# Softplus as one ScalarE function in a planned selective-scan block, with the planner's priorities shifted

## The chip, the core and the metric

The kernel runs on one core of a Trainium2 chip. The core has a matrix engine (TensorE, PE in the profile; PEld is its weight load), VectorE (DVE), ScalarE (ACT), GpSimd (POOL) and SyncE (SP), whose queue issues all DMAs here. The metric is the device time of one execution in microseconds; before the change it is 3109.58 us (median of 3 runs, 3109.41 to 3114.28).

## The reference, cut to what matters

The input x is 2 sequences of 2048 tokens with 1024 channels, float32 throughout. Three blocks follow each other, each on a layernorm of x and added to x: a routed feed-forward block (FFN 1), a selective scan with 16 states per channel, and the same feed-forward block again (FFN 2).

```python
xz = jnp.einsum('btd,rd->btr', x, W_xproj)
delta_r, B_mat, C_mat = xz[..., :r], xz[..., r:r + n], xz[..., r + n:]
delta = jax.nn.softplus(jnp.einsum('btr,dr->btd', delta_r, W_dt) + b_dt)
A = -jnp.exp(A_log)
dA = jnp.exp(delta[..., None] * A)
Bu = delta[..., None] * B_mat[:, :, None, :] * x[..., None]
# scan over t: h = dA_t * h + Bu_t;  y_t = sum_n h * C_t
return y + x * D_param
```

`delta` holds the step sizes of the title: one per token and channel. The feed-forward block forms 64 vectors of rank 16 per token (`vecs`), keeps the 4 longest, and adds their product with a second weight to x W + bias.

## The kernel before, in words

Tokens are worked in 16 chunks of 256 (`TC`), each chunk in two tiles of 128 rows for the FFNs. `ffn("f", c, i)` is FFN 1 of tile i of chunk c, `ffn("g", c, i)` is FFN 2. An FFN tile has three stages of products on TensorE, each 2 halves x 8 matmuls of 128x512 (`products`, line 578; each float32 matmul leaves two records in the profile): with `wa` into two PSUM banks `pv`, with `ww` into two banks `po`, and with `wb` into the same `po`. Between the first and the last stand the squares (ACT, line 631), the choice (`choose`, `routed`, `total`; DVE, lines 645 to 668), `spread` (POOL, line 677), eight transposes on TensorE (line 560) and the copies that bring them to SBUF (ACT, line 565, tile `gt`). `close` (DVE, line 695) adds the result to x. The layernorm is folded in: the weights wa and ww are centred once at the start, and the row's own scale comes in `close`, from `stats` (DVE, lines 512 to 527) and `root` (ACT, lines 532 to 534).

`prepare(c)` normalises and transposes the chunk, projects it, and computes `delta`. Here lie the lines that the change touches. For each half g of the channels (32 groups in all) four matmuls (`pz`, line 797) give z in two PSUM banks, taken one after the other. Then comes softplus(z) = max(z, 0) + ln(1 + exp(-|z|)), with a term that keeps what rounding loses in 1 + e: Abs and Relu on ACT out of PSUM with the bias of the channel (`parts`, lines 806 and 807), Exp (819), three steps on DVE (`plus` 822, `one` 827, `rest` 830), Ln on ACT (833), and a subtraction on DVE (`delta`, 836). `times` (840) multiplies by u, and two DMAs (856) write delta and delta x u to DRAM. ACT loads a function table whenever the function needed isn't in the active one (ACT_TABLE_LOAD).

`scans(c)` reads them back, repeated over partitions (`rep`), and does 64 steps per chunk: `decay` (Exp on ACT into one of two PSUM buffers `da`, line 917), `entry` (DVE, 925), `scan` (DVE, 932), `keep` (ACT, 942), `leave` and `join` (POOL, 945 and 964), and for each two channel blocks a sum over states on TensorE (974) and `skip` (DVE, 988 and 991).

The order of work is not written by hand: every piece is a `Task` with an engine, a cost, what it reads and writes, and a `rank`. `Plan.order` plays the tasks through in time with these costs. Each engine takes the ready task of the lowest rank that finds its buffers; the order that results is what each engine executes, strictly in that order, waiting on semaphores. A buffer taken with `spare=1` asks for one more free place than it takes. Tasks marked `port` are not planned on DVE and POOL at the same time. There are five PSUM banks in the pool `bank`. FFN 1 runs up to three chunks ahead of the scans.

At the start SyncE loads the transposed x tile (`load_t`), the weights wa, ww, the first x tile in rows (`load`, rank -1006.8), half_bias, wb and the rest (ranks -1009 to -1003). DVE adds the row blocks of wa (`gather`, line 447), POOL those of ww. TensorE turns these sums into column means (`mean`, line 472, rank -1000) and corrects the first tile, whose products use the weights not yet centred (`correct`, 461, rank -1400). DVE subtracts the means (`center`, 482, rank -900).

Of the kernel before, what the change touches and what calls it, by code (L numbers as in the profile page):

```python
# [31 lines left out]

class Place:
# [10 lines left out]
class Task:  # L64
    __slots__ = (
        "eng", "cost", "emit", "rank", "take", "give", "port", "land", "turn", "waits", "users", "n",
        "at",
# [9 lines left out]
class Plan:  # L77
# [15 lines left out]
    def add(  # L93
        self, eng, cost, emit, reads=(), writes=(), rank=0.0, take=(), give=(), port=False, land=0.0,
        turn=None,
    ):
        t = Task()
        t.eng, t.cost, t.emit, t.rank = eng, cost, emit, rank
        t.take, t.give, t.port, t.land, t.turn = take, give, port, land, turn
        t.users, t.n = [], len(self.tasks)  # L100
        before = set()
        for key in reads:
            if key in self.written:
                before.add(self.written[key])
            self.readers.setdefault(key, []).append(t.n)
        for key in writes:
            if key in self.written:
                before.add(self.written[key])
            before.update(self.readers.get(key, ()))
            self.written[key] = t.n  # L110
            self.readers[key] = []
        for p in take:
            p.taker = t.n
        for p in give:
            p.users += 1
        for key in (*reads, *writes):
            if isinstance(key, tuple) and isinstance(key[0], Place):
                before.add(key[0].taker)
        before.discard(t.n)
        t.waits = len(before)  # L120
        for n in before:
            self.tasks[n].users.append(t.n)
        self.tasks.append(t)
        return t

    def order(self):
# [9 lines left out]
        def arrive(t):  # L136
            heapq.heappush(ready[t.eng], (t.rank() if callable(t.rank) else t.rank, t.n))
# [89 lines left out]
def macaron_kernel(  # L227
# [179 lines left out]
    def load_all():  # L407
        def one(dst, src, key, us, rank):
            keys = [(*key, h) for h in range(2)] if isinstance(key, tuple) else [key]
            add("SP", us, lambda: nc.sync.dma_start(out=dst, in_=src), [], keys, rank=rank, land=3.6)  # L410

        def big(w_sb, w, name, rank):
# [10 lines left out]
            rank=-1000.0, take=[mean_w])  # L423
# [17 lines left out]
        for w_sb, name, key in ((wa, "wa", "pv"), (ww, "ww", "po")):  # L441
            total = Place("row" if name == "wa" else "delta")
            for k in range(1, KC):
                def gather(k=k, w_sb=w_sb, total=total):
                    t = flat(total)
                    eng = nc.vector if total.pool == "row" else nc.gpsimd
                    eng.tensor_add(t, w_sb[:, 0, :] if k == 1 else t, w_sb[:, k, :])

                add("DVE" if name == "wa" else "POOL", 1.01 if name == "wa" else 2.45, gather, [(name, 0, 0), (name, k, 0)], [(total, 0)], rank=-1000.0,
                    take=[total] if k == 1 else [], port=True)  # L450
# [17 lines left out]
            for h in range(2):  # L468
                pt = Place("bank")

                def mean(h=h, total=total, pt=pt):
                    nc.tensor.matmul(
                        pt.tile, lhsT=mean_w.tile[:, :P], rhs=flat(total)[:, h * HD : (h + 1) * HD], start=True,
                        stop=True,
                    )

                add("PE", 0.41, mean, [(total, 0), (mean_w, 0)], [(pt, 0)], rank=-1000.0, take=[pt],
                    give=[total, mean_w])
                for k in range(KC):
                    def center(k=k, h=h, w_sb=w_sb, pt=pt):  # L480
                        part = w_sb[:, k, h * HD : (h + 1) * HD]
                        nc.vector.tensor_sub(part, part, pt.tile)  # L482

                    add("DVE", 0.49, center, [(pt, 0)], [(name, k, h)], rank=-900.0, give=[pt])
# [6 lines left out]
            [], ["half_bias"], rank=272.6)  # L491
# [15 lines left out]
    def spread_of(x_p, st, factor, rank, after=()):  # L507
# [28 lines left out]
        add("DVE", 1.95, stats, row(x_p) + list(after), [(st, 0)], rank=-109.8 + rank, take=[st])  # L536
        add("ACT", 2.64, root, [(st, 0)], [(st, 1)], rank=72.4 + rank)
# [14 lines left out]
    def turn(src, keys, dst, out_keys, rank, take=(), give_src=None):  # L552

        for g in range(2):
# [9 lines left out]
            def act(g=g, pt=pt):  # L564
# [4 lines left out]
                give=[src] if give_src else [])  # L569
            add("ACT", 0.58, act, [(pt, 0)], out_keys(g), rank=-111.3 + rank, give=[pt])  # L570
# [3 lines left out]
    def products(turn_of, ps, h, lhs, w, wn, start, stop, order, take, give, after=()):  # L574
        for k4 in range(KC // 4):
            def pe(k4=k4):
# [12 lines left out]
                [(ps[h], 0)], turn=turn_of, rank=order, take=take if k4 == 0 else (), give=give)  # L589

    def ffn(kind, c, i):
# [21 lines left out]
        for h in range(2):  # L613
            def bias(h=h):
                cols = slice(h * HD, (h + 1) * HD)
                nc.gpsimd.tensor_add(x_p.tile[:, cols], x_p.tile[:, cols], half_bias[:, cols])  # L616

            add("POOL", 1.12, bias, row(x_p, h) + ["half_bias"], row(x_p, h), rank=rank, port=True)
# [7 lines left out]
        for h in range(2):  # L626
# [3 lines left out]
            def square(h=h):  # L630
# [7 lines left out]
                take=[g_p] if h == 0 else [])  # L638

        def choose():  # L640
# [14 lines left out]
            take=[ch, mk], give=[mk])  # L655
        for h in range(2):
            def routed(h=h):
# [7 lines left out]
                give=[pv[h]])  # L665
# [7 lines left out]
        add("DVE", 1.2, total, [(g_p, 0), (g_p, 1)], [(ch, 1)], rank=-45.5 + rank)  # L673
        for h in range(2):
            def spread(h=h):
# [8 lines left out]
                give=[ch])  # L684
# [5 lines left out]
        for h in range(2):  # L690
            products(turn_of, po, h, gt, wb, "wb", False, True, lambda: turn_of.number - 1000.0, [], [gt])

            def close(h=h):
# [7 lines left out]
                rank=-286.1 + rank, give=[po[h], st])  # L701
        if kind == "f":
            x1_ds[c, i] = x1_d = Place("x1_d")

            def keep():
# [3 lines left out]
                land=2.5)  # L709
# [11 lines left out]
    def prepare(c):  # L721
# [48 lines left out]
        def keep(p, pt, m):  # L770
# [4 lines left out]
            give=[pd])  # L775
        add("PE", 0.93, project_bc, ["wx"] + u_all, [(pb, 0)], rank=-79.8 + rank, take=[pb])
        add("ACT", 0.46, keep(bc, pb, P), [(pb, 0)], [(bc, 0)], rank=-138.9 + rank, take=[bc],
            give=[pb])
        add("PE", 0.36, fold, [(bc, 0)], [(pf, 0)], rank=91.8 + rank, take=[pf])
        add("ACT", 0.54, keep(bc, pf, 2 * N), [(pf, 0)], [(bc, 0)], rank=104.1 + rank, give=[pf])  # L780
# [8 lines left out]
        for g in range(2):  # L789
            dg, e = Place("delta"), Place("row")  # L790
            for k2 in range(HC // 2):
                pt = Place("bank")

                def pz(g=g, k2=k2, pt=pt):
                    for k in range(2):
                        kc = g * HC + 2 * k2 + k
                        nc.tensor.matmul(  # L797
                            pt.tile[:, k * TC : (k + 1) * TC], lhsT=wdt[:, kc * P : (kc + 1) * P],
                            rhs=dr.tile, start=True, stop=True,
                        )  # L800

                def parts(g=g, k2=k2, pt=pt, e=e, dg=dg):
                    for k in range(2 * k2, 2 * k2 + 2):
                        bias = bdt[:, g * HC + k : g * HC + k + 1]
                        z = pt.tile[:, k % 2 * TC : (k % 2 + 1) * TC]
                        nc.scalar.activation(e.tile[:, k * TC : (k + 1) * TC], z, AF.Abs, bias=bias)
                        nc.scalar.activation(dg.tile[:, k, :], z, AF.Relu, bias=bias)

                add("PE", 1.01, pz, [(dr, 0), "wdt"] + ([(e, "-")] if k2 else []), [(pt, 0)],
                    rank=-186.8 + rank, take=[pt] if k2 else [pt, e, dg], give=[dr])  # L810
                add("ACT", 1.95, parts, [(pt, 0), "bdt"], [(e, k2), (dg, k2)], rank=66.7 + rank,
                    give=[pt])
            ek, dk = [(e, k) for k in range(HC // 2)], [(dg, k) for k in range(HC // 2)]

            def flat(dg):
                return dg.tile.rearrange("p k t -> p (k t)")

            def exp(e=e):
                nc.scalar.activation(e.tile, e.tile, AF.Exp, scale=-1.0)

            def plus(e=e, dg=dg):
                nc.vector.scalar_tensor_tensor(
                    flat(dg), flat(dg), -1.0, e.tile, ALU.mult, ALU.subtract
                )

            def one(e=e):
                nc.vector.tensor_scalar_add(e.tile, e.tile, 1.0)

            def rest(e=e, dg=dg):
                nc.vector.scalar_tensor_tensor(flat(dg), e.tile, -1.0, flat(dg), ALU.add, ALU.add)  # L830

            def log(e=e):
                nc.scalar.activation(e.tile, e.tile, AF.Ln)

            def delta(e=e, dg=dg):
                nc.vector.tensor_sub(flat(dg), e.tile, flat(dg))
# [6 lines left out]
            add("ACT", 1.15, exp, ek, ek, rank=-3.2 + rank)  # L843
            add("DVE", 1.41, plus, ek + dk, dk, rank=-132.6 + rank, port=True)
            add("DVE", 0.92, one, ek, ek, rank=-214.4 + rank, port=True)
            add("DVE", 1.19, rest, ek + dk, dk, rank=-159.7 + rank, port=True)
            add("ACT", 3.62, log, ek, ek, rank=11.7 + rank)
            add("DVE", 1.21, delta, ek + dk, dk, rank=-94.7 + rank, port=True, give=[e])
            add("DVE", 1.07, times, dk + ukeys, ukeys, rank=-43.2 + rank, port=True, give=[dg])
            for s in range(2):  # L850
# [7 lines left out]
                add("SP", 0.4, put, (ukeys if s else dk), [(du_d, g, s)] + (["prepare"] if g and s else []),  # L858
# [3 lines left out]
    def scans(c):  # L862
# [20 lines left out]
        for q in range(0, KC, 2):  # L883
# [26 lines left out]
            for odd in range(2):  # L910
                for j, hi in [(j, hi) for j in range(odd, NJ, 2) for hi in range(HI)]:
# [45 lines left out]
                    add("ACT", 0.17, keep, [(h, 0)], [key, (h, 1)], rank=-239.7 + rank)  # L957
# [14 lines left out]
            def total(sums=sums, y=y):  # L972
# [10 lines left out]
                give=sums)  # L983
# [24 lines left out]
    for c in range(NCH):  # L1008
# [3 lines left out]
        if chunks[c][1] == 0:  # L1012
            add("POOL", 0.36, lambda: nc.gpsimd.memset(state, 0.0), [],
                [("state", q, j, hi) for q in range(0, KC, 2) for j in range(NJ) for hi in range(HI)],
                rank=63.8)
# [64 lines left out]
```

## Time and profile before

| what | before |
|---|---|
| median of 3 runs | 3109.58 us |
| span of the profiled execution | 3105.1 us |
| busy PE / DVE / ACT / POOL | 3054.2 / 2816.7 / 1869.4 / 2364.5 us |
| PE records | 9020 |
| ACT_TABLE_LOAD | 65 x 1283 ns (32 at line 833, 31 at line 917, 2 single ones) |
| mean granted TensorE clock | 0.998 |

The profile is of one execution, and it gives its span, from the first instruction to the last; the median of the runs is 4.5 us longer than that span. A line of a group reads: line, engine, operation, out<-in, shapes, count | busy us, mean ns of one | idle time of the engine just before, with what ended it. A line of waits reads: who waited for whom: us in total, times, longest. A line of a timeline reads: start, duration, engine, line, operation, count, and in brackets the idle time before it. In a table of stretches each line gives the busy time of every engine between two moments.

### The profile page before, as it was taken

What the parts mean: (1) busy time and instruction counts of PE and PEld (TensorE: products, weight loads), DVE (VectorE), ACT (ScalarE), POOL (GpSimd) and SP (SyncE); (2) the same over time, 40 slices, a digit from 0 to 9 for tenths busy, and PEclk for the clock granted to TensorE, in tenths of its full rate; (3) what the DMA queues carried; (4) which work ended last, traced back from release to release, by engine and by line L of the source; (5) the groups of instructions that cost most, each with busy time, mean ns of one, the idle gap of its engine ahead of it and who ended that gap; (6) DMA issues with size and microseconds to landing.
All of it is one profiled execution on the core that took longest, in us unless ns stands there. A gap on an engine that the chain in (4) does not pass through costs nothing.

```text
span 3105.1 us, 36153 instructions
## 1 busy us (share of the span) xinstructions
PE 3054.2 (98%) x9020; PEld 1409.4 (45%) x9020; DVE 2816.7 (91%) x4683; ACT 1869.4 (60%) x4851; POOL 2364.5 (76%) x1882
## 2 busy tenths in 40 slices
PE   8999999999999999999999999999999999999999
PEld 3444444444444444444444444444444444444444
DVE  4279999999999999999999999999999999997951
ACT  1366666656666676666566665666557675565531
POOL 3148787888788788788887887878888788886861
PEclk9999999999999999999999999999999999999999
DMA  5154654646465465555555555555465555544630
GB/s 226 61 167 147 194 146 138 195 142 190 130 183 157 145 181 163 154 159 163 166 172 150 165 162 164 166 166 169 133 172 168 166 161 148 160 143 130 170 81 14
DMA packets 408371, 478.69 MB, mean 154 GB/s; under 512 B 161504, under 2 KB 253280, under 8 KB 408160
## 3 DMA queue, kind: packets, MB, share of 16 engines
q1 hardware_dynamic: 408160, 476.37, 52.6%
q8 instruction: 72, 1.18, 0.2%
q14 instruction: 139, 1.14, 0.1%
HBM read 375.07 MB, written 101.19 MB: 153 GB/s over the span
## 4 chain that ended last, share of the span: by engine, by line
PE 60%; DVE 24%; issue 6%; ACT 4%; DMA 2%; POOL 2%; SPq 0%; DVEq 0%; POOLq 0%; ACTq 0%
PE bank L578 53%; DVE h L932 10%; DVE h L925 5%; PE bank L974 2%; PE bank L560 2%; PE bank L748 1%; POOL h L945 1%; DVE g L658 1%; ACT da L917 1%; DVE norms L645 1%; PE bank L797 1%; DVE stats L512 1%; DMA rep<-du_d 1%; DVE choice L652 1%; DVE bank L988 1%
## 5 line engine op out<-in xcount | busy, mean ns | idle before, releaser
L945 POOL TENSOR_TENSOR h<-h,c 128x512 f32<-128x512 f32 x1024 | 1323.7, 1303 | 351.8 <-ACT state L942 316.8
L917 ACT ACTIVATE da<-rep,a_neg 128x256 f32<-128x256 f32 x2048 | 974.8, 477 | 725.4 <-DVE h L932 675.6
L932 DVE TENSOR_TENSOR_SCAN h<-da,state,h 128x256 f32<-128x256 f32 x2048 | 1404.8, 731 | 7.3 <-ACT da L917 5.5
L578 PE MATMUL bank<-wa,xnt 128*128 128x512 f32 x2048 | 905.6, 596 | 5.4 <-DVE wa L482 4.0
L578 PE MATMUL bank<-wb,gt 128*128 128x512 f32 x2048 | 895.9, 595 | 10.0 <-ACT gt L565 9.8
L578 PE MATMUL bank<-ww,xnt 128*128 128x512 f32 x2048 | 889.4, 592 | 0.0
L964 POOL TENSOR_TENSOR h<-h,h 128x512 f32<-128x512 f32 x512 | 654.7, 1279 | 40.1
L925 DVE TENSOR_TENSOR h<-rep,b 128x512 f32<-128x512 f32 x1024 | 670.2, 665 | 12.5 <-ACT b L879 6.7
L578 PEld LDWEIGHTS bank<-ww,xnt 128*128 128x128 f32 x2048 | 389.1, 190 | 489.8 <-issue 483.4
L578 PEld LDWEIGHTS bank<-wb,gt 128*128 128x128 f32 x2048 | 384.4, 190 | 485.2 <-issue 453.5
L578 PEld LDWEIGHTS bank<-wa,xnt 128*128 128x128 f32 x2048 | 384.9, 191 | 483.4 <-issue 470.8
L677 POOL TENSOR_TENSOR g<-choice 128x512 f32<-128x512 f32 x128 | 143.5, 1142 | 195.8 <-DVE choice L668 195.8
L942 ACT COPY state<-h 128x2 f32<-128x2 f32 x1024 | 187.9, 185 | 54.5 <-DVE h L932 53.3
L631 ACT ACTIVATE g<-bank 128x512 f32<-128x512 f32 x128 | 133.8, 1047 | 87.9 <-PE bank L578 55.6
L512 DVE BATCH_NORM_STATS2 stats<-xf 128x6 f32<-128x512 f32 x128 | 81.2, 676 | 57.4 <-DMA xf<-in_x 57.4
L616 POOL TENSOR_TENSOR xf<-xf,half_bias 128x512 f32<-128x512 f32 x64 | 81.1, 1287 | 66.4 <-DVE stats L512 66.3
L974 PE MATMUL bank<-h,summer 128*32 128x512 f32 x1024 | 123.1, 598 | 0.0
L645 DVE TENSOR_REDUCE norms<-g 128x64 f32<-128x1024 f32 x64 | 77.0, 1203 | 50.8 <-ACT g L631 49.4
L533 ACT ACTIVATE stats<-stats,pads 128x1 f32<-128x1 f32 x288 | 111.3, 387 | 9.7
L565 ACT COPY gt<-bank 128x512 f32<-128x512 f32 x128 | 71.4, 592 | 66.9 <-PE bank L560 66.4
L695 DVE SCALAR_TENSOR_TENSOR xg<-bank,stats,xg 128x512 f32<-128x512 f32 x64 | 47.4, 741 | 67.6 <-PE bank L578 67.2
L532 ACT ACTIVATE stats<-stats 128x1 f32<-128x1 f32 x288 | 58.1, 202 | 81.8 <-DVE stats L527 75.7
(84 smaller groups left out, 1969.2 us busy)
## 6 DMA issues: line engine op xcount, KB each, us to landing
rep<-du_d SPq DMA_DIRECT2D x1024, 256.0 KB, 3.7
xnt<-in_x_t SPq DMA_DIRECT2D x32, 512.0 KB, 4.1
xf<-in_x SPq DMA_DIRECT2D x32, 512.0 KB, 5.4
x_d<-xf SPq DMA_DIRECT2D x32, 512.0 KB, 3.3
u_d<-u SPq DMA_DIRECT2D x32, 512.0 KB, 4.7
ysb<-u_d SPq DMA_DIRECT2D x64, 256.0 KB, 3.4
du_d<-delta SPq DMA_DIRECT2D x32, 512.0 KB, 3.2
du_d<-u SPq DMA_DIRECT2D x32, 512.0 KB, 3.5
```

Of the source, the lines that this page charges most:

```text
L512: nc.vector.bn_stats(st.tile[:, 6 * s : 6 * s + 6], x_p.tile[:, s * HD : (s + 1) * HD])
L533: nc.scalar.activation(t, q, AF.Identity, bias=less, scale=hv)
L578: nc.tensor.matmul(ps[h].tile, lhsT=lhs.tile[:, k, :], rhs=w[:, k, h * HD : (h + 1) * HD], start=start and k == 0, stop=stop and k == KC - 1,)
L631: nc.scalar.activation(g_p.tile.rearrange("p (a r) -> p r a", r=RANK)[:, h * r2 : (h + 1) * r2, :], vecs(pv, h), AF.Square,)
L677: nc.gpsimd.tensor_mul(g_p.tile[:, h * HD : (h + 1) * HD].rearrange("p (r a) -> p r a", a=na), ch.tile[:, :NA].unsqueeze(1).to_broadcast([ ...
L917: nc.scalar.activation(da.tile[:, k, :], r.tile[:, k, 0, :], AF.Exp, scale=a_neg[:, q + k, j, hi : hi + 1],)
L925: nc.vector.tensor_mul(h.tile, r.tile[:, :, 1, :], bs[hi].tile.unsqueeze(1).to_broadcast([P, 2, TC]),)
L932: nc.vector.tensor_tensor_scan(h.tile[:, k, :], da.tile[:, k, :], h.tile[:, k, :], state[:, q + k, j, hi : hi + 1], ALU.mult, ALU.add,)
L942: nc.scalar.copy(state[:, q : q + 2, j, hi : hi + 1], h.tile[:, :, TC - 1 : TC])
L945: nc.gpsimd.tensor_mul(h.tile, h.tile, cs[hi].tile.unsqueeze(1).to_broadcast([P, 2, TC]))
L964: nc.gpsimd.tensor_add(first.tile, first.tile, h.tile)
L974: nc.tensor.matmul(y.tile[j // 2 * 2 * DB : (j // 2 + 1) * 2 * DB, :], lhsT=summer[:, DB * (1 - j % 2) : DB * (3 - j % 2)], rhs=sums[j].ti ...
```

## The change

The eight steps of a softplus group become one task of four `Softplus` activations on ACT, which read z from two PSUM banks with the bias and write `delta`. The four matmuls before them become one task that takes both banks at once (each with `spare=1`). Four DVE steps, Exp and Ln of the group, and the scratch tile `e` go. Every task gets a tag, and a table `SHIFT` adds a number per tag to its rank, so that all engines' orders differ from before.

```diff
+SHIFT = {
+    "load_t": -196.3,
+    "load": 140.4,
+    "load_w": 106.3,
...
+    "correct": 469.1,
+    "mean": -922.8,
+    "center wa": 659.8,
+    "gather ww": 528.1,
+    "center ww": -330.7,
...
+    "stats xf 0.5": 409.2,
...
+    "turned g": -572.4,
+    "products ww": -448.6,
+    "products wb": 147.3,
...
+    "root xf 1.0": 1757.6,
...
+    "pz": -3.0,
+    "softplus": 0.8,
...
+    "decay": 158.5,
+    "entry": 670.3,
+    "scan": -114.3,
...
+}
...
-            heapq.heappush(ready[t.eng], (t.rank() if callable(t.rank) else t.rank, t.n))
+            rank = t.rank() if callable(t.rank) else t.rank
+            heapq.heappush(ready[t.eng], (rank + SHIFT.get(t.tag, 0.0), t.n))
...
-            dg, e = Place("delta"), Place("row")
-            for k2 in range(HC // 2):
-                pt = Place("bank")
...
+            dg, pts = Place("delta"), [Place("bank", spare=1) for _ in range(HC // 2)]
+
+            def pz(g=g, pts=pts):
+                for k in range(HC):
+                    kc = g * HC + k
+                    nc.tensor.matmul(
+                        pts[k // 2].tile[:, k % 2 * TC : (k % 2 + 1) * TC],
+                        lhsT=wdt[:, kc * P : (kc + 1) * P], rhs=dr.tile, start=True, stop=True,
+                    )
+
+            add("PE", 2.02, pz, [(dr, 0), "wdt"], [(pt, 0) for pt in pts],
+                rank=-186.8 + rank, take=[*pts, dg], give=[dr])
+
+            def softplus(g=g, pts=pts, dg=dg):
+                for k in range(HC):
+                    nc.scalar.activation(
+                        dg.tile[:, k, :], pts[k // 2].tile[:, k % 2 * TC : (k % 2 + 1) * TC],
+                        AF.Softplus, bias=bdt[:, g * HC + k : g * HC + k + 1],
+                    )
+
+            add("ACT", 4.6, softplus, [(pt, 0) for pt in pts] + ["bdt"], [(dg, 0)],
+                rank=11.7 + rank, give=pts)
...
-            add("ACT", 1.15, exp, ek, ek, rank=-3.2 + rank)
-            add("DVE", 1.41, plus, ek + dk, dk, rank=-132.6 + rank, port=True)
-            add("DVE", 0.92, one, ek, ek, rank=-214.4 + rank, port=True)
-            add("DVE", 1.19, rest, ek + dk, dk, rank=-159.7 + rank, port=True)
-            add("ACT", 3.62, log, ek, ek, rank=11.7 + rank)
-            add("DVE", 1.21, delta, ek + dk, dk, rank=-94.7 + rank, port=True, give=[e])
-            add("DVE", 1.07, times, dk + ukeys, ukeys, rank=-43.2 + rank, port=True, give=[dg])
+            add("DVE", 1.07, times, [(dg, 0)] + ukeys, ukeys, rank=-43.2 + rank, port=True, give=[dg])
```

## The prediction

> **What bounds the kernel now.** I read the busy row of the page and the chain that ended last, then a table of stretches, then TensorE's own waits.
>
> ```profile
> PE 3054.2 (98%) x9020; PEld 1409.4 (45%) x9020; DVE 2816.7 (91%) x4683; ACT 1869.4 (60%) x4851; POOL 2364.5 (76%) x1882
> ...
> PE 60%; DVE 24%; issue 6%; ACT 4%; DMA 2%; POOL 2%; SPq 0%; DVEq 0%; POOLq 0%; ACTq 0%
> ```
>
> TensorE (PE) is busy for all but 51 us of a span of 3105.1. The stretches are: loading; the first tiles of FFN 1; the body with scans; the last scans; the last FFN tiles.
>
> ```profile
> core 0: us, PE busy (x) PEld busy (x) DVE busy (x) ACT busy (x) POOL busy (x), PEclk, DMA share, GB/s
> 0.00:50.00 50.00, 36.24 (x82) 17.35 (x83) 31.22 (x51) 6.76 (x15) 25.51 (x29) 0.90 0.87 330
> 50.00:170.00 120.00, 119.24 (x334) 57.16 (x333) 33.04 (x70) 35.81 (x89) 14.07 (x12) 1.00 0.19 66
> 170.00:2800.00 2630.00, 2601.89 (x7788) 1201.36 (x7787) 2558.94 (x4247) 1710.92 (x4458) 2159.33 (x1710) 1.00 0.56 161
> 2800.00:2990.00 190.00, 188.11 (x529) 84.51 (x528) 173.16 (x278) 100.81 (x258) 147.12 (x117) 1.00 0.51 140
> 2990.00:3105.10 115.10, 108.77 (x292) 49.02 (x290) 20.35 (x40) 15.09 (x34) 18.48 (x16) 1.00 0.13 35
> ```
>
> Subtract: PE idles 13.8 us while loading (clock 0.90), 0.8 in the second stretch, 28.1 in the body, 1.9 and 6.3 at the end. VectorE (DVE) is also nearly full in the body (2558.9 of 2630, 97%), but has little to do in the outer stretches. PE works through all five, so its queue sets the end, and an edit that spares other engines can win only PE's idle time.
>
> In the body PE waits mostly for short ScalarE copies that bring transposes out of PSUM:
>
> ```profile
> PE bank L578 <- ACT gt L565: 9.0, 19, 1.7
> PE bank L560 <- ACT xnt L565: 4.9, 6, 2.0
> ```
>
> **The change, part by part.** PE keeps its 256 step-size matmul records (line 797, 61.9 us), now issued eight at a time. What goes and comes is on the other engines:
>
> ```profile
> L807 ACT ACTIVATE delta<-bank,bdt 128x256 f32<-128x256 f32 x128 | 61.0, 476 | 0.0
> L806 ACT ACTIVATE row<-bank,bdt 128x256 f32<-128x256 f32 x128 | 60.4, 472 | 14.1 <-PE bank L797 14.1
> ...
> L833 ACT ACT_TABLE_LOAD x32 | 41.1, 1283 | 0.6
> ...
> L917 ACT ACT_TABLE_LOAD x31 | 39.8, 1283 | 0.6
> ```
>
> *ScalarE (ACT).* Gone: Abs 60.4, Relu 61.0, Exp (line 819) 33.6, Ln 33.8 = 188.8 us. New: 128 Softplus. None is in the trace. Lower bound: the 357 to 476 ns of any 128x256 step here (copies of line 771 take 370). Upper bound: twice 476, if it needed two passes. I take 476, the row with the same shape, PSUM source and pointer bias, because Exp and Ln also cost the same here (1050 and 1057 on 128x1024). That is 61 us (46 to 122), so ACT loses 128 us (67 to 143).
>
> *Table loads.* Ln already forces a load, and the next Exp of the scans a load back: 32 + 31, 1283 ns each. A Softplus with a table of its own needs the same pair, so I count no difference. Bounds: all gone, -81 us; one more pair per group, +82 us, all on an engine that is idle for 40% of the span.
>
> The Trainium skill, "ScalarE: Activation LUTs", "Rules for kernel authors", speaks against the edit: Exp and Ln together should use one set that holds both, with a single load. By that rule the kernel before had nothing to lose and the edit would add some 82 us of loads. The trace shows the 63 loads already there, so the row decides. The same page, "What ACT_TABLE_LOAD costs", adds a drain of about 1380 ns to each switch. No run here shows it: Ln begins as its load ends (load at 1827.57 for 1.28 us, Ln at 1828.86).
>
> *VectorE.* Lines 822 (1398 ns), 827 (770), 830 (1253), 836 (1320) go: 4741 ns x 32 = 151.7 us. Its load falls to 2665 us, in the body from 97% to about 92%. These four also held the port that the planner keeps from GpSimd. As PE, not DVE, has the work until the end, I count none of the 151.7 directly. They count only through PE's body waits, which copies in ACT's queue and late DVE results cause. All of these would give 28.1 + 1.9 = 30 us. I take 9 of them, a third: more slack on two engines should shorten waits, but most are the bare latency of a copy (9.0 us over 19 is 0.47 us each, the copy itself 0.59), which nothing in the edit shortens. Bounds: 25 of the 30, and on the other side what the first rival costs.
>
> *Queues.* A softplus task keeps ACT for 1.28 + 4 x 0.476 = 3.2 us (4.5 with the load back), and then come state copies, `gt` copies and decays. The Ln task now keeps it for 2.3 (3.6 with the load back). DVE has two `da` buffers, 2 x 2 x 0.73 + 0.67 = 3.6 us with one entry multiply between, so a block of 4.5 can cost it about 0.9 us x 32 = 29 us, less than the 152 spared. On SyncE the two writes per group stay, and the first comes earlier, after Softplus instead of after line 836.
>
> *Order at the start.* This is where the shifts act in a place that can be read. Now, on PE, `correct` (-1400) goes ahead of `mean` (-1000). On DVE the statistics of the first x tile stand ahead of `center wa`, and that tile lands only at 27.7 (timeline of the start; L461 is `correct`, L472, at 24.37 and again at 39.35, is `mean`):
>
> ```profile
> 22.66 1.88 PE L461 MATMUL bank<-row,part 128*128 128x512 f32 x4
> ...
> 27.68 1.29 DVE L512 BATCH_NORM_STATS2 stats<-xf 128x6 f32<-128x512 f32 x2 [10.22 <-DMA xf<-in_x]
> ...
> 29.56 9.65 DVE L482 TENSOR_TENSOR wa<-wa,bank 128x512 f32<-128x512 f32 x16
> ...
> 30.29 5.38 PE L578 MATMUL bank<-wa,xnt 128*128 128x512 f32 x8 [4.04 <-DVE wa L482]
> ```
>
> With the shifts `mean` is -1922.8, `correct` -930.9, `center wa` -240.2, the statistics +299.4. The x load (-866.4) leaves SyncE after all weights (-902.7 to -896.7), so near 40 us instead of 17.4. `mean` then needs only the column sums (VectorE's additions of line 447 end at 17.45), not the products before it; centring can begin near 19 to 23 instead of 29.6, and the 4.04 us wait goes. With it goes its aftermath: the eight records at 30.29 take 5.38 us, where eight at 49.48 take 3.60, so they run slow by 1.8. The second wait, ahead of ww's `mean` at 39.35, is 3.68 us for the last centring and then 1.56 for a bank, and the eight records after it, at 43.87, take 5.34, 1.7 more than 3.60: 7.0 in all. It moves forward too, but ww's column sums end on GpSimd only at 35.8. I take all of the first (5.8) and somewhat less than half of the second (3.2): 9. Bounds: 12.8; and nothing, if `mean` stands on PE ahead of products and waits there for the sums. The late x tile is covered: landing about 10 us after its issue as before, near 50, it is needed when the tile closes, after its wb products, which start at 66.65 now. If DVE stands waiting for it, the next tile's selection is late, with 28 us of ww and wb products as cover on PE.
>
> **Sum.** 3105.1 - 9 (start) - 9 (body) + 0 (end: the last two tiles' products stand behind the last state sums as now) = 3087.1. The median of the runs is 4.5 us above the profiled span, so about **3092 us**, 0.6% less.
>
> **Rivals.**
> *Two banks for the whole softplus makes PE wait (slower).* Now each two step-size products take one of five PSUM banks, released by two ACT steps. In the new form two banks are taken together and kept until the fourth Softplus, 1.9 us of PE (8 records x 61.9 / 256) plus 3.2 of ACT plus its queue, and the task wants a third bank free, as do the next tile's wa products. For it: five banks, of which a tile in its wb stage holds two. If PE stands for the ACT part, 3.2 us x 32 = 102 us; if a half is covered by other products, 51, less the 18 gained: 3110 + 51 - 18 = 3143. It decides from 18/32 = 0.6 us per group. Against it: the planner lets PE take other ready tasks, and PE has always had some (98%).
> *The gain stays away (same).* The start gives back a wait in another place and body waits are bare latencies: 3105 to 3114, I put it at 3109.
> *DVE was a co-bound (faster by more).* 97% busy in the body and 24% of the chain: if PE's waits are all due to DVE's lateness, 25 of the 30 go, and 12.8 at the start: 3105.1 - 37.8 + 4.5 = 3072.
> *It does not do what it says.* If copies, squares or Identity are not in Softplus's table, loads multiply: 128 more are 164 us on ACT, which has 1236 idle; PE's copies would come later by 1.3 us each time, some 20 to 40 us: 3135. The loads before show copies between an Ln and the next load, so copies do not need one there.
>
> **Numbers.** Forecast 3092 (3079 to 3103): 0.50. Larger gain 3072: 0.11. Same: 0.15. Two banks 3143: 0.20. More loads 3135: 0.04. Faster by over 0.2% (about what this kernel's measurement can tell from no change) 0.61, within it 0.15, slower 0.24. The range that leaves out some 2 in 10: 3070 to 3138, holding most of the larger gain and the near half of the slower cases.
>
> **What would show it.** In the profile after: lines 806 to 836 gone from ACT and DVE, a Softplus group of 128 near 476 ns, 32 loads at it and some 31 at the scans' Exp; PE's time while loading up from 36.2 to about 45 of 50; PE idle in the body near 20 us; DVE near 2665 in all. I am wrong if PE waits for Softplus or for a bank at what stands for line 797, if PE's body idle grows beyond 39 us (which eats the start's 9), or if the load count is far from 65.

## The result, and the profile after

The changed kernel takes 3214.43 us (median of 4 runs, 3213.32 to 3218.92) against 3111.64 for before, a ratio of 1.0331 with a 95% interval of 1.0316 to 1.0346: 103 us slower where 18 us faster was forecast, and outside the range of 3070 to 3138.

The page of the changed kernel, in the lines that answer to those of before:

```profile
PE 3079.6 (96%) x9020; PEld 1421.9 (44%) x9020; DVE 2730.6 (85%) x4555; ACT 1772.3 (55%) x4655; POOL 2335.4 (73%) x1882
...
DVE 45%; PE 33%; issue 8%; ACT 7%; DMA 5%; POOL 1%; SPq 1%; DVEq 0%; POOLq 0%; ACTq 0%
```

Every engine but TensorE does less, and VectorE's share of the chain that ended last went from 24 to 45%. The same stretches as in the prediction show where the time went:

```profile
0.00:50.00 50.00, 41.92 (x108) 20.53 (x109) 33.03 (x47) 6.83 (x9) 23.00 (x27) 1.00 0.87 330
50.00:170.00 120.00, 119.76 (x333) 57.39 (x332) 30.56 (x71) 34.82 (x90) 16.43 (x14) 1.00 0.25 81
170.00:2800.00 2630.00, 2515.70 (x7488) 1161.77 (x7487) 2447.28 (x4064) 1596.61 (x4212) 2095.70 (x1678) 0.99 0.54 159
2800.00:2990.00 190.00, 185.45 (x527) 82.83 (x530) 180.14 (x298) 103.28 (x280) 168.77 (x137) 1.00 0.49 138
2990.00:3211.50 221.50, 216.82 (x572) 99.35 (x564) 39.61 (x78) 30.79 (x65) 31.49 (x27) 1.00 0.13 35
```

The first column after the length is PE. While loading it is busy 41.9 us instead of 36.2, and at a granted clock of 1.00 instead of 0.90: by 170 us it has worked 441 records where it had worked 416 (the counts behind the busy times). In the body it idles 114.3 us (2630 - 2515.7) instead of 28.1. VectorE thins out near 2990 us, as before, but the matmuls that TensorE did not do in the body then remain, and the last stretch is 221.5 us long instead of 115.1. The account closes: idle of PE over the span 131.9 instead of 50.9 us (+81.0), busy time +25.4 (the `wb` products alone 921.2 instead of 895.9; the mean granted clock is 0.988 instead of 0.998, so records run slower), together 106.4, the difference of the two spans.

TensorE's waits over the whole span of the changed kernel (who for whom: us, times, longest):

```profile
PE bank L623 <- ACT gt L628: 38.6, 25, 5.3
PE bank L642 <- ACT gt L628: 24.5, 13, 4.4
PE bank L623 <- POOL g L743: 16.6, 14, 7.3
```

They are not the short waits for a copy any more: a wait for a gt copy took 0.47 us on average before and takes 1.5 and 1.9 now, and single waits reach 7.3 us. One wait of 3.4 us is for Softplus (line 871). What the longest for a gt copy, 5.3 us, hangs on can be followed in the timeline (some lines of it):

```profile
507.62 1.39 DVE L967 TENSOR_TENSOR_SCAN h<-da,state,h 128x256 f32<-128x256 f32 x2
508.93 1.26 DVE L573 BATCH_NORM_STATS2 stats<-xf 128x6 f32<-128x512 f32 x2
...
510.90 0.20 ACT L593 ACTIVATE stats<-stats 128x1 f32<-128x1 f32 x1 [0.76 <-DVE stats L588]
...
513.52 0.29 ACT L595 ACTIVATE stats<-stats 128x1 f32<-128x1 f32 x1
513.72 0.57 ACT L628 COPY gt<-bank 128x512 f32<-128x512 f32 x1
```

The statistics stand on VectorE behind a row of scans, ScalarE's `root` waits for the statistics, the copy stands on ScalarE behind `root`, and TensorE goes on at 514.34. So here a late VectorE holds TensorE through the order of a third engine. One row of the page says where the lateness begins, the scan's, before and then after:

```profile
L932 DVE TENSOR_TENSOR_SCAN h<-da,state,h 128x256 f32<-128x256 f32 x2048 | 1404.8, 731 | 7.3 <-ACT da L917 5.5
```

```profile
L967 DVE TENSOR_TENSOR_SCAN h<-da,state,h 128x256 f32<-128x256 f32 x2048 | 1404.8, 734 | 71.5 <-ACT da L952 4.0
```

The scans are as long as ever, but VectorE now stands 71.5 us ahead of them, of which the row puts only 4.0 down to another engine. The rest is VectorE waiting for itself. A few steps of its timeline, before and then after:

```profile
1035.34 0.66 DVE L925 TENSOR_TENSOR h<-rep,b 128x512 f32<-128x512 f32 x1
1035.92 1.39 DVE L932 TENSOR_TENSOR_SCAN h<-da,state,h 128x256 f32<-128x256 f32 x2
1037.22 0.66 DVE L925 TENSOR_TENSOR h<-rep,b 128x512 f32<-128x512 f32 x1
1037.80 1.39 DVE L932 TENSOR_TENSOR_SCAN h<-da,state,h 128x256 f32<-128x256 f32 x2
```

```profile
498.56 0.66 DVE L960 TENSOR_TENSOR h<-rep,b 128x512 f32<-128x512 f32 x1
499.32 1.39 DVE L967 TENSOR_TENSOR_SCAN h<-da,state,h 128x256 f32<-128x256 f32 x2
500.63 0.66 DVE L960 TENSOR_TENSOR h<-rep,b 128x512 f32<-128x512 f32 x1
501.39 1.39 DVE L967 TENSOR_TENSOR_SCAN h<-da,state,h 128x256 f32<-128x256 f32 x2
```

A step is 1.88 us before (1037.22 - 1035.34) and 2.07 after. Before, the scan starts 0.58 us after the entry ahead of it, while that entry (0.66 long) is still ending; after, 0.76, behind its end. The program shows why. The buffers' numbers in four instructions of this kind (from the instruction lists, earlier in the scans than the lines above), before and after:

```
L925 TensorTensor h_97<-rep_81        L960 TensorTensor h_90<-rep_80
L932 scan h_89                        L967 scan h_90
L925 TensorTensor h_90<-rep_82        L960 TensorTensor h_94<-rep_81
L932 scan h_97                        L967 scan h_94
```

Before, an entry stands ahead of the scan of the step before it; after, each scan follows the entry that writes its own buffer. Counted over the starts in the two traces: of some 760 places where a scan directly follows an entry, 23 have a pitch (from start to start) of 700 to 850 ns before, and 644 after (medians 579 and 766). 644 x 0.187 us is 120 us of VectorE time that the planner doesn't know of. About 104 ns of a long pitch show as idle time; the rest is the overlap of the entry's end with the next start, which is gone.

Laid beside the order that the kernel's own `Plan.order` makes, the traces also tell which of these scans read what the entry ahead of them wrote: 15 of 758 before, 668 of 760 after. In the changed kernel none of the 668 starts within 690 ns, while 88 of the other 92 start within 600 (median 598; by that figure the price is 168 ns, or 108 us). The source of these pairs is two entries of the shift table, `"entry": 670.3` and `"scan": -114.3`: entries go last, so none is taken ahead of need. Played through without both, the planner leaves 94 such pairs of 853 (in a far longer plan, as the other shifts were chosen with these two); without either one alone, 689 and 668 stay.

### The profile page after: what moved, and what is told of

The parts are those of the page before. It is cut to its first block, busy times and chain, and to the rows that moved or that the text cites. A ratio compares the mean times of both kernels' runs of the same rounds, so it can differ in the third digit from the quotient of the medians.

```text
span 3211.5 us, 36179 instructions
## 1 busy us (share of the span) xinstructions
PE 3079.6 (96%) x9020; PEld 1421.9 (44%) x9020; DVE 2730.6 (85%) x4555; ACT 1772.3 (55%) x4655; POOL 2335.4 (73%) x1882
## 4 chain that ended last, share of the span: by engine, by line
DVE 45%; PE 33%; issue 8%; ACT 7%; DMA 5%; POOL 1%; SPq 1%; DVEq 0%; POOLq 0%; ACTq 0%
PE bank L642 29%; DVE h L967 23%; DVE h L960 10%; ACT da L952 2%; DVE stats L573 2%; DVE g L724 2%; DMA xf<-in_x 2%; DMA rep<-du_d 2%; DVE norms L711 2%; DVE choice L734 1%; PE bank L623 1%; ACT stats L594 1%; PE bank L1009 1%; DVE bank L1023 1%; DVE choice L718 1%
## 5 line engine op out<-in xcount | busy, mean ns | idle before, releaser
L980 POOL TENSOR_TENSOR h<-h,c 128x512 f32<-128x512 f32 x1024 | 1302.3, 1280 | 420.7 <-ACT state L977 376.7
L967 DVE TENSOR_TENSOR_SCAN h<-da,state,h 128x256 f32<-128x256 f32 x2048 | 1404.8, 734 | 71.5 <-ACT da L952 4.0
L642 PE MATMUL bank<-wb,gt 128*128 128x512 f32 x2048 | 921.2, 609 | 24.7 <-ACT gt L628 24.5
L642 PEld LDWEIGHTS bank<-wb,gt 128*128 128x128 f32 x2048 | 395.2, 196 | 510.6 <-issue 470.4
L681 POOL TENSOR_TENSOR xg<-xg,half_bias 128x512 f32<-128x512 f32 x64 | 81.0, 1268 | 78.7 <-PE bank L623 77.7
L458 POOL TENSOR_TENSOR xg<-yt,xg 128x512 f32<-128x512 f32 x64 | 82.3, 1286 | 56.6 <-DMA yt<-y_d 56.6
```

What stands on the lines that cost most here:

```text
L642: nc.tensor.matmul(ps[h].tile, lhsT=lhs.tile[:, k, :], rhs=w[:, k, h * HD : (h + 1) * HD], start=start and k == 0, stop=stop and k == KC - 1,)
L967: nc.vector.tensor_tensor_scan(h.tile[:, k, :], da.tile[:, k, :], h.tile[:, k, :], state[:, q + k, j, hi : hi + 1], ALU.mult, ALU.add,)
L980: nc.gpsimd.tensor_mul(h.tile, h.tile, cs[hi].tile.unsqueeze(1).to_broadcast([P, 2, TC]))
```

## The experiments

Theory O: the new order costs the time. Theory B: the two banks held through Softplus. Theory S: Softplus itself and its loads.

### Softplus in the order of before

```diff
-                        nc.scalar.activation(e.tile[:, k * TC : (k + 1) * TC], z, AF.Abs, bias=bias)
-                        nc.scalar.activation(dg.tile[:, k, :], z, AF.Relu, bias=bias)
+                        nc.scalar.activation(dg.tile[:, k, :], z, AF.Softplus, bias=bias)
...
-                nc.scalar.activation(e.tile, e.tile, AF.Exp, scale=-1.0)
+                pass
...
```

(plus, one, rest, log and delta likewise do nothing.)

> Softplus takes the place of Abs and Relu, two activations per PSUM bank, and Exp, Ln and the four VectorE steps go; every engine keeps the order of the kernel before for all that is left, and banks are taken one at a time. Theory O (the new order is what costs: it fits the planned durations, and on the chip results come later than TensorE's turn for them): 3085 to 3112 us, TensorE's idle time in the body (170 to 2800 us) at most 28 us as before. Theory B (two banks taken at once and held through Softplus): the same, 3085 to 3112, since one bank is taken here. Theory S (Softplus itself, with its table loads and its stay on ScalarE, holds TensorE's copies up): above 3170, and body idle over 90 us.

3112.46 us, ratio 1.0003 (0.9994 to 1.0012). Its page and its body stretch:

```profile
PE 3058.5 (98%) x9020; PEld 1411.4 (45%) x9020; DVE 2677.2 (86%) x4555; ACT 1818.5 (58%) x4705; POOL 2324.1 (75%) x1882
```

```profile
170.00:2800.00 2630.00, 2596.66 (x7748) 1198.33 (x7747) 2425.12 (x4119) 1659.64 (x4306) 2111.74 (x1702) 1.00 0.55 161
```

Theory S falls: Softplus in place of the chain costs nothing on balance. It brings nothing either: VectorE's busy time is 139.5 us lower, and PE idles 33.3 us in the body where it idled 28.1. Theories O and B are both just missed, by 0.5 us of time and 5 us of idle time. With two tasks per group there are 55 + 55 loads instead of 32 + 31, and VectorE waits 78.4 us for `da` (5.5 before); what this would have cost without the time that the chain freed, no run shows.

### The old chain under the new shifts

The four functions and four VectorE steps of before, put back into the changed kernel, with its shifts; the planner plans anew.

> The softplus chain of the kernel before (Abs, Relu, Exp, Ln, four VectorE steps, one bank at a time) planned with the changed kernel's table of shifts. Theory O: slower than before by more than 2%, above 3175 us, although neither Softplus nor the pair of banks is there. Theories B and S: near 3110, at most 3130, as what they blame is absent.

3355.41 us, ratio 1.078 (1.0763 to 1.0796). The shifts cost without Softplus, which speaks against B and S; 633 of 706 entry-scan neighbours are of the long kind. But the planner made another order for these tasks, and a poor one by its own costs: its planned span is 3283.2 us, where it plans 3119.6 for the kernel before and 3108.6 for the changed one. Most of this loss was in the plan, so it isn't the lateness that theory O means, and the size says little about the change itself.

### One bank at a time under the new shifts

```diff
-                rank=-186.8 + rank, take=[*pts, dg], give=[dr])
...
+                    rank=-186.8 + rank, take=[pt] if k2 else [pt, dg], give=[dr])
...
-                rank=11.7 + rank, give=pts)
...
+                    rank=11.7 + rank, give=[pt])
```

> The changed kernel with its shifts, but one bank at a time: two matmuls into one bank, then a task of two Softplus activations that frees it, without the spare bank. The planner plans anew. Theory B: most of the loss goes, 3090 to 3140 us, TensorE's body idle under 50. Theory O: the loss stays, 3160 to 3260, with TensorE still waiting for gt copies and for the spread on GpSimd. Theory S: 3180 to 3260, with up to twice the table loads.

3253.49 us, ratio 1.0457 (1.0443 to 1.0471); 658 of 771 neighbours are long. Theory B expected most of the loss to go; it grew. This order too is another one (planned span 3157.1 us), and PE waits 15.9 us for Softplus in it, so it clears the banks only as the main cause. Loads were 32 + 32, not twice as many.

### The changed kernel with less VectorE work

```diff
-                                h.tile[:, k, :],
-                                da.tile[:, k, :],
-                                h.tile[:, k, :],
+                                h.tile[:, k, : TC * 7 // 8],
+                                da.tile[:, k, : TC * 7 // 8],
+                                h.tile[:, k, : TC * 7 // 8],
```

> The changed kernel, every order untouched, but each scan works on 224 of its 256 columns (this leaves out an eighth of the scan), which takes about 0.17 us of VectorE from each of 1024 steps, some 175 us in all. Theory O in the form that VectorE runs late against the plan that made the order: TensorE's body idle of 114 us falls below 60 and the time below 3150 us. Theory B and theory S: body idle stays above 90 and the time above 3185, since no bank is freed sooner and ScalarE's work is the same.

3112.77 us, ratio 1.0005 (0.9995 to 1.0014), with every order and both banks as in the changed kernel. The scans' busy time fell from 1404.8 to 1267.9 us, by 137 instead of the 175 expected:

```profile
170.00:2800.00 2630.00, 2583.23 (x7751) 1194.29 (x7750) 2418.01 (x4217) 1642.67 (x4358) 2180.07 (x1747) 0.99 0.56 165
```

PE's body idle is 46.8 us. Theory O, in the form that VectorE is late against the plan, holds, and theory B as the main cause falls. What makes VectorE late was not yet shown, as less work helps against any lateness. The neighbours of the timeline gave theory D: the dependent pair. Against it stood R: other causes.

### Only the neighbours parted

In the changed kernel the list that the planner returns is edited: a scan directly behind its own entry goes behind the next entry, if that follows on VectorE and nothing between needs the scan or its `da`. Nothing else moves.

```diff
-    for t in plan.order():
+    for t in apart(plan.order()):
```

> The changed kernel with one thing different in VectorE's order: a scan that stood directly behind its own entry multiply goes behind the entry multiply that comes next, so that the two that depend on each other are no longer neighbours; all other engines keep their order, all work is done. Theory D (in the changed order most scans follow their own entry at once, and VectorE then starts the scan 766 ns after the entry began instead of 579; some 760 such pairs are 142 us that the planner doesn't know of, and TensorE waits for what is late): the pitch from entry to scan falls back to about 580 ns, TensorE's body idle below 60 us, the time to 3090 to 3130 us. Rival theory R (the short scan helped only because VectorE had less work; the lateness has other causes, such as ScalarE's queue or the port shared with GpSimd): the time stays above 3180.

3122.46 us, ratio 1.0037 (1.0025 to 1.005): 92 of the 103 us are gone with all work, all banks and all other orders as in the change. Of 672 neighbours 58 are long, and VectorE stands 12.1 us ahead of its scans instead of 71.5. PE's body idle is 54.9 us: half of what it was, but still twice the 28.1 of before. Its body stretch and two lines of its timeline, the pitch 0.58 us again:

```profile
170.00:2800.00 2630.00, 2575.15 (x7734) 1191.08 (x7734) 2484.82 (x4206) 1638.33 (x4346) 2174.49 (x1742) 1.00 0.56 164
```

```profile
1509.89 0.66 DVE L960 TENSOR_TENSOR h<-rep,b 128x512 f32<-128x512 f32 x1
1510.47 1.38 DVE L967 TENSOR_TENSOR_SCAN h<-da,state,h 128x256 f32<-128x256 f32 x2
```

### The kernel before with its neighbours put together

The counter-test: in the kernel before, an entry directly ahead of another step's scan goes behind that scan.

> The kernel before, computation and all, with one thing different in VectorE's order: an entry multiply that stood directly ahead of another step's scan goes behind that scan, so that most scans now follow their own entry at once. Theory D: VectorE, 97% busy in the body, gets some 100 to 140 us more to do, the pitch from entry to scan goes from 579 to about 766 ns, and the time to 3180 to 3250 us, without Softplus and without the shifts. Theory R: within 1% of before, below 3140.

3183.92 us, ratio 1.023 (1.0214 to 1.0246), with no Softplus and no shifts. 382 of 544 neighbours are long, 359 more than before; 359 x 0.187 is 67 us (fewer pairs than the 100 to 140 us expected), and 74 were lost.

```profile
170.00:2800.00 2630.00, 2554.92 (x7551) 1177.55 (x7550) 2506.90 (x4128) 1667.36 (x4327) 2108.07 (x1657) 0.99 0.54 157
```

PE idles 75.1 us there instead of 28.1. Theory D stands by both tests, R falls.

### An order that knows of it

If the order is what counts, an order chosen with the pair in its costs should let Softplus's savings be used. The planner gets a few lines, and a table of shifts is searched with them (for tasks of one bank; `exp`, `log` and the four VectorE steps stay in the plan at a quarter of their cost and do nothing):

```diff
+        last = {}
...
+                    name, own = t.emit.__name__, t.emit.__defaults__
+                    if name == "scan" and last.get(e) is own[0]:
+                        t.cost += 0.19
+                    last[e] = own[1] if name == "entry" else None
```

> Softplus one bank at a time (as in the first experiment), with another table of shifts, chosen for a planner that charges 0.19 us to a scan that directly follows its own entry multiply. All work is done. Theory D: few such pairs are left, TensorE waits less than in the kernel before, 3085 to 3108 us. Theory R: an order made for planned durations is late on the chip again, above 3130.

3079.32 us, ratio 0.9896 (0.9883 to 0.991), better than both kernels; 37 of 840 neighbours are long.

```profile
PE 3045.9 (99%) x9020; PEld 1407.7 (46%) x9020; DVE 2673.5 (87%) x4555; ACT 1812.5 (59%) x4701; POOL 2332.3 (76%) x1882
```

```profile
170.00:2800.00 2630.00, 2610.70 (x7823) 1206.91 (x7822) 2447.79 (x4160) 1674.20 (x4348) 2141.58 (x1718) 1.00 0.56 163
```

PE idles 19.3 us in the body and is busy 42.6 of the first 50 us. By 170 us it has worked 442 records (416 before, 441 in the changed kernel), so some 10 of the 33 us won lie at the start. No order was searched for these tasks without the charge, so that the charge was needed to find it isn't shown.

> The same new order on every engine, but with the softplus chain of the kernel before in it (Abs, Relu, Exp, Ln, four VectorE steps in their places). If the order alone brings the gain of the kernel beside it, this one is within 0.3% of that; if the 140 us that Softplus spares VectorE are needed for it, this one is slower by 0.5 to 4%, since the order was chosen with a quarter of their cost.

3222.22 us, ratio 1.0355 (1.034 to 1.0369): the same order with the old chain is 143 us slower than with Softplus, 4.6%, a little more than expected. So this order alone brings no gain; it needs the time that Softplus frees. An order searched for the old chain with the pair in its costs was not tried.

> Softplus one bank at a time, a third table of shifts, chosen in the same way but with half of the old chain's cost kept in the plan, which leaves VectorE more room than the plan shows. Theory D: 3090 to 3112 us. Theory R: above 3130.

3097.93 us, ratio 0.9954 (0.9941 to 0.9966): this table holds too, with less gain. PE's body idle is 30.4 us, no less than before, so its gain lies outside the body.

## Why the prediction was wrong

**What bounds the kernel: right but incomplete.** PE's queue sets the end before and after. But that bound holds only if the results come in the order and at the times for which PE's own order was made.

**The step that failed** is VectorE's: "I count none of the 151.7 directly", and "I take 9 of them, a third: more slack on two engines should shorten waits". PE's idle time in the body did not fall by 9, it rose by 86, with 25 us of slow records on top. The step took it that the work left on VectorE keeps its price when it is put in another order. It did not: 644 of the pairs became 187 ns dearer, 120 us, and an order made without them left PE waiting. VectorE's busy time shows it as well: 2730.6 us where the prediction had 2665. The third of the body waits was not there for the taking either: in the old order Softplus gave 1.0003, and it took an order searched for the new tasks to bring the body's idle time to 19.3 us. That this is 8.8 less than before, near the 9 of the prediction, doesn't confirm it: it came with an order other than the one that the prediction was for.

**The shifts were read at the start only.** `entry` and `scan` stood in the diff with +670 and -114, and the order that they make on VectorE can be worked out by playing `Plan.order` through. The trace of before has a hint of the price too: the scans behind their own entry, 15 in all, start there at a median of 723 ns, and 720 of the other 743 within 600. (Of the 23 long pitches before, 10 are not such pairs.)

**Start: right.** The 9 us were idle time and the slow records after it. Idle time while loading fell by 5.7 us, and with the clock at 1.00 the records are not slow: the 25 more that TensorE has worked by 170 us are, but for one, wa products, which follow each other at 0.43 us, so some 10 us of work. Centring began at 19.3 us instead of 29.6, and the 4.04 us wait went. In its place `mean` waits on PE for the column sums, which the prediction named as the bound:

```profile
18.13 1.99 PE L533 MATMUL bank<-row,part 128*128 128x512 f32 x4 [1.65 <-DVE row L508]
19.30 9.66 DVE L543 TENSOR_TENSOR wa<-wa,bank 128x512 f32<-128x512 f32 x16 [1.22 <-PE bank L533]
```

**Softplus and its loads: right.** 474 ns each where 476 was taken, and 30 + 30 loads where 32 + 31 were expected:

```profile
L871 ACT ACTIVATE delta<-bank,bdt 128x256 f32<-128x256 f32 x128 | 50.5, 474 | 16.8 <-PE bank L861 16.2
```

```profile
L871 ACT ACT_TABLE_LOAD x30 | 38.5, 1283 | 0.5
L952 ACT ACT_TABLE_LOAD x30 | 38.5, 1283 | 0.5
```

The group's mean times its count would be 60.7; it is busy for 50.5, as activations that follow each other overlap. ScalarE's busy time fell by 97 us where 128 was taken, inside the bounds. The 29 us that a block of ScalarE could cost VectorE did not come: 4.0 us of waits for `da`.

**The rival "two banks" had the direction right for a wrong reason.** Its 3143 is 71 us short, and that its uncovered 102 us equal the loss of 103 is luck. With both banks held as in the change and only the neighbours parted, 92 of the 103 us went. The some 12 us that remain are a balance: the start gained some 10, and what the banks and the other orders cost against that was not split. That stays open. "More loads" and "DVE a co-bound" did not happen; VectorE's 97% did mean something else, that an order on it can't be made longer for free.

The Trainium skill, "VectorE: DVE Perf Modes", "The DRAIN you can't avoid", says that the next VectorE operation does not start until the pipeline is empty, that one that is not held starts earlier, and that in a chain of copies a semaphore after each cost nothing extra. For this pair the runs show a cost: the same scan starts 579 ns after an entry that it does not depend on and 766 after its own. "Perfetto Trace Analysis", "Optimizing Scalar/DVE Operations", says that the write-acknowledgement half of an instruction's profiled latency overlaps with the next instruction, which fits the 579; the timelines show that overlap gone when the next one reads what is being written.

## What to carry to other kernels

Read every shift of a new order as the neighbours that it makes on each engine, above all on the one nearest to full: here two VectorE operations that depend on each other should have an independent one between them (measured for an entry and its scan; other pairs and engines were not). An order fits the durations it was chosen with: price the same order with its real durations before trusting it, and when work is removed, choose the order again with the price of the pair in the model. An engine that is idle 15% of the time can still be the cause, if the others wait for it in turn.

## What the runs showed of the hardware

A VectorE scan that directly follows the multiply which writes its input starts 187 ns later than behind another multiply (766 and 579 ns after that multiply's start, in the changed kernel and in the one before). The profile puts some of this time, 71.5 us ahead of the scans, down as idle, nearly all without a releaser. And between Softplus and the Exp of the scans the table is loaded anew each way here: 30 loads into it and 30 back, 1283 ns each. Without a loss in the end (1.0003), the first experiment had 55 + 55 of them, and 78 us of waits for the scans' `da`.
